# Input rows of an attention layer loaded in two-row parts, and the statistics rows asked for one unit earlier

## The chip, the cores and the metric

The kernel runs on one core of a Trainium2 chip. Its measure is the device time in microseconds (us) of one execution: 2961.36 us, the median of three runs (2960.82 to 2961.66). The engines of the core are named as the profile names them: PE is TensorE's matrix multiply and PEld its weight load, DVE is VectorE, ACT is ScalarE, POOL is GpSimd, SP is SyncE, which here only issues transfers. An engine followed by q (SPq) is its sequencer.

## The reference

The input x is 2 images of 128 channels by 256 x 256 pixels in float32 (a row of all channels is 128 KB). Two layers follow each other, each a normalisation over groups of four channels, a function, and the addition of the layer's input:

```python
x = x + attention(group_norm(x))   # layer 0: 8x8 windows, keys of a 12x12 halo, 4 heads, fixed mask
x = x + convolutions(group_norm(x))   # layer 1: 5x1, then 3x1 by channel, times a 3-tap product
```

In layer 0 the pixels are projected to queries, keys and values with a 384 x 128 matrix; a window of 8 x 8 queries attends to the 12 x 12 keys around it, with relative position terms, a mask that leaves only keys of the query's own row and column parity, and a softmax; the result is projected with a 128 x 128 matrix. A group's mean and variance go over 4 channels and all 65,536 pixels, so no pixel of an image can be normalised before all of it has been read once.

## The kernel before

Both layers go over an image in 32 strips of 8 rows, so there are 64 strips. In layer 0 a strip `k` has two units, `u = 2k + r`, one for even and one for odd rows (the mask keeps them apart); 128 units follow each other. One unit is a fixed sequence on PE: biases (L562), scores (L579), keys of a later unit (L382), coefficients (L473), weighted values (L605), then in an even unit (r = 0) the values of the next strip (L495), in an odd unit the queries of two units (L445, L447), and the output projection (L382). All engines run in the order in which the program was written: the loop stands in `manual_schedule(engines=ORDERED)`, so nothing is moved by a scheduler. A transfer that SP issues waits for all that SP has been told before it.

What SP is told in layer 0, in order:

- even unit: `load_rows(k + 2)`, the ten input rows of the strip after next (L316, 1280 KB, tile `f_raw`, three buffers); after `values` the transfers of `bring(0, ...)` (L525, L529, L532), which copy the values from one SBUF tile (`f_vn`) into the places from which L605 reads them (`f_vt`); then the store of this unit's result (L643, 512 KB).
- odd unit: `load_next()` (L305), then `bring(1, ...)` after `attend`, then the store.

`load_next` serves the statistics of the second image: while the first image is attended, its rows are read into a single buffer (`f_sx`) and VectorE takes their sums (`input_stats`, L128). This is done 29 times, ten rows each in the first 12 and eight rows each in the other 17, in the even units 2 to 58 (`stats_at`). The buffer is filled again from the odd unit after that. The rows of the first image are read for statistics before the loop (L266), at the start of the kernel.

A `bring` has six transfers, or twelve where the strip's four key rows are put in two pieces. With three strips to a turn, the twelve-transfer `bring(1, ...)` falls into units 3, 9, 15 and so on, just ahead of the even units 4, 10, 16. Each transfer of SP counts on one of eight semaphores in turn, and waits until the transfer before it on that semaphore has landed.

A unit's `normalise(k + 2)` (DVE, L356) in the odd unit reads the ten rows that were asked for in the even unit before it. Layer 1 has loads and stores of its own and isn't touched by the change.

Of the kernel before, what the change touches and what calls it, by code (L numbers as in the profile page):

```python
# [187 lines left out]
def attention_fast(tc, io, x1_d, norm, st_x, st_y, tags, ends, weights, both, layer1):  # L188

    nc = tc.nc  # L190
    x = io["x"]
# [3 lines left out]
    with ExitStack() as l0:  # L195
# [43 lines left out]
        with ExitStack() as setup:  # L239
# [24 lines left out]
            for s in range(NS):  # L264
                t = sp.tile([P, 8, W], F32, tag="sx", name=f"f_sx_0_{s}")
# [16 lines left out]
        stats_at, norm_at = {}, {}  # L282
        quarter_at = {}
        for b in range(NB - 1):
            row = 0
            for i in range(NS - 3):
                n = 10 if i < 12 else 8
# [9 lines left out]
        coming, sxs = sorted(stats_at), {}  # L297

        def load_next():
            if coming:  # L300
                u = coming.pop(0)
                b, row, n = stats_at[u]
                t = rawp.tile([P, 10, W], F32, tag="sx", name=f"f_sx_{b}_{row}", bufs=1)
                sxs[u] = t[:, 0:n]
                nc.sync.dma_start(sxs[u], x[b, :, row : row + n, :])  # L305

        def input_stats(u):
            b, row, n = stats_at[u]
# [2 lines left out]
        def load_rows(k):  # L311

            b, s = divmod(k, NS)
            t = rawp.tile([P, 10, W], F32, tag="raw", name=f"f_raw_{k}")
            n = min(10, H - 8 * s)
            nc.sync.dma_start(t[:, 0:n, :], x[b, :, 8 * s : 8 * s + n, :])  # L316
            raws[k] = t

        def slots_of(k):

            first = (4 * k + 2) % 6
            return [(0, 4, first)] if first < 4 else [(0, 2, 4), (2, 2, 0)]
# [78 lines left out]
        def keys(u, first=TWO, second=TWO):  # L401
            k, r = divmod(u, 2)
            s = k % NS
            keys_r = by_window(r)

            def part(c):
                pk = ps_pj.tile([P, 512], F32, tag="pj", name=f"f_pk_{u}_{c}")
                in_parts(second if c else first, pk, wkT, xn[k % 2][:, :, r, c].rearrange("p n i j -> p n (i j)"))
                for i, m, slot in slots_of(k):
                    nc.scalar.copy(  # L410
                        keys_r[:, c, :, 8 * slot : 8 * (slot + m)],
                        pk.rearrange("p (n x) -> p n x", n=NPAIR)[:, :, 8 * i : 8 * (i + m)],
                    )
                if c:
                    for i, m, slot in slots_of(k):
                        beside(r, slot, m)

            def top():

                pk = ps_pj.tile([P, 512], F32, tag="pj", name=f"f_pk_{u}_top")  # L420
                for c in range(2):
                    nc.tensor.matmul(
                        pk[:, W * c : W * c + W], wkT,
                        tops[k // NS][1][:, :, r, c].rearrange("p n i j -> p n (i j)"), start=True, stop=True,
                    )
                slot = (4 * k) % 6
                nc.scalar.copy(
                    keys_r[:, :, :, 8 * slot : 8 * slot + 16],
                    pk.rearrange("p (c n x) -> p c n x", c=2, n=NPAIR),
                )  # L430
                beside(r, slot, 2)

            return ([top] if s == 0 else []) + [lambda c=c: part(c) for c in range(2)]
# [70 lines left out]
        def top_values(b):  # L504

            flat, _, v = tops[b]
            for g in range(2):
                pv = ps_pj.tile([P, 512], F32, tag="pj", name=f"f_pv_top_{b}_{g}")
                for n in range(4):
                    nc.tensor.matmul(  # L510
                        pv[:, P * n : P * n + P], flat[:, P * (4 * g + n) : P * (4 * g + n) + P], wvT,
                        start=True, stop=True,
                    )
                (nc.vector.tensor_copy if g % 2 else nc.scalar.copy)(
                    v[:, 4 * g : 4 * g + 4, :, 0:32], pv.rearrange("p (n h d) -> p n h d", n=4, h=HEADS)
                )
# [19 lines left out]
        def bring_top(r, b):  # L536

            v, slot = tops[b][2], 4 * NS * b % 6
            for c in range(2):
                for odd in range(2):  # L540
                    lo, to = 64 * odd + 16 * (2 * r + c), 64 * c
                    nc.sync.dma_start(
                        vt[r][to + 8 * slot : to + 8 * slot + 16, c, odd:NPAIR:2], v[lo : lo + 16]
                    )
                    first = to + 48 + 2 * slot
                    nc.sync.dma_start(
                        vt[r][first : first + 3 : 2, c, odd + 1 : NPAIR : 2], v[lo + 7 : lo + 16 : 8, 0 : 8 - odd]
                    )
                    nc.sync.dma_start(
                        vt[r][first + 1 : first + 4 : 2, c, 1 - odd : NPAIR - 1 : 2],  # L550
                        v[lo : lo + 9 : 8, 1 - odd : 8],
                    )
# [98 lines left out]
        def emit(parts):  # L651
            for f in parts:
                f()

        load_rows(0)
        load_rows(1)
        weights.load()
        with tc.manual_schedule(engines=ORDERED):
            normalise(0)
            emit(keys(0, ONE, ONE))  # L660
            top_values(0)
            bring_top(0, 0)
            values(0, range(4))
            for r in range(2):
                bring(r, slots_of(0))
            bring_top(1, 0)
            by_place(0, (0, 4))
            coefficients(0, 0)
            coefficients(0, 1)
            normalise(1)  # L670
            by_place(1, (0, 2))
            for u in range(2):
                emit(queries(u, ONE, ONE))
            for u in range(NU):
                k, r = divmod(u, 2)
                b, s = divmod(k, NS)
                later, more = u + 1 < NU, k + 1 < NB * NS
                if r == 0:
                    if k + 2 < NB * NS:
                        load_rows(k + 2)  # L680
                elif k + 2 < NB * NS:
                    normalise(k + 2)
                if u in stats_at:
                    input_stats(u)
                if u == 0 or u - 1 in stats_at:
                    load_next()
                step = lambda: None
                if u in norm_at:
                    st, i, name = norm_at[u]
                    steps = norm.steps(st[i], ps_pj, name, last=False)  # L690
                    step = lambda: next(steps)
                if u == 8:
                    weights.sums()
                if u in (NU - 4, NU - 2, NU - 1):
                    next(layer1)
                biases(u)
                scores(u, pieces(u)[3])
                step()
                step()
                at_top = more and (k + 1) % NS == 0  # L700
                cuts = pieces(u)[0]
                if later:
                    emit(keys(u + 1, cuts, cuts))
                step()
                step()
                if more:
                    coefficients(k + 1, r)
                elif later:
                    next(layer1)
                step()  # L710
                attend(u)
                if more and r == 1:
                    bring(1, slots_of(k + 1))
                    if at_top:
                        bring_top(1, b + 1)
                if not later:
                    next(layer1)
                turn(u)
                step()
                if r == 0 and more:  # L720
                    if at_top:
                        top_values(b + 1)
                        bring_top(0, b + 1)
                    values(k + 1, range(4))
                    bring(0, slots_of(k + 1))
                elif later and more:
                    cuts = pieces(u)[1]
                    emit(queries(u + 1, cuts, cuts) + queries(u + 2, cuts, cuts))
                if more and r == 0:
                    by_place(k + 1, (2, 4))  # L730
                elif k + 2 < NB * NS:
                    by_place(k + 2, (0, 2))
                if u > 0:
                    result_stats(u - 1)
                project(u)
                if u in quarter_at:
                    st, i, name, part = quarter_at[u]
                    norm.quarter(st[i], name, part)
                del qs[u]
            result_stats(NU - 1)  # L740
# [966 lines left out]
```

## Time and profile before

| | |
|---|---|
| median of three runs | 2961.36 us |
| the profiled execution, its own time | 2962.31 us |
| its span, first to last instruction | 2960.0 us |
| granted PE clock, mean | 0.993 |
| layer 0, from unit 0 to the start of unit 127 | 113.27 to 1955.97 us |
| PE busy in that stretch | 1771.95 of 1842.70 us |
| DVE, ACT, POOL busy in that stretch | 1149.15, 894.61, 560.92 us |
| share of DMA time in that stretch, rate | 0.56, 150 GB/s |
| rest, layer 1: PE busy | 989.84 of 1004.03 us |

How to read it: the span is one execution as the hardware profiler saw it. Busy times of engines overlap. The instructions that PE and PEld execute are counted apart (51,762 each). A wait of an engine is put down to what ended it; "issue" means that nothing the profile shows ended it. In the list of DMA queues, q1 carries what SP issues, q0 what POOL issues, and q8 and q14 carry instructions to the engines. In answers on stretches of time, each number before a bracket is busy time of an engine in us.

### The profile page before, as it was taken

Reading aid. Unit: us, or ns where it says so; the run is one execution under the profiler, and the core shown is the slowest. Engines: PE = TensorE matmul, PEld = TensorE weight load, DVE = VectorE, ACT = ScalarE, POOL = GpSimd, SP = SyncE. Lnnn points to the kernel's source line nnn. Section 1 sums busy time; section 2 is a strip of 40 time slices with the busy share of each in tenths; the row PEclk is TensorE's granted clock in tenths of the full one; section 3 lists DMA queues with packets and bytes.
Section 4 is the critical chain, followed back from the end, with each engine's and each line's share of the span. In section 5 each row is a group of like instructions: output and inputs, shape, how many; then the busy total and the mean of one; then the engine's idle time right before and its main releaser. Section 6 shows DMA issues by size and latency. Waiting matters only on the chain.

```text
span 2960.0 us, 117321 instructions
## 1 busy us (share of the span) xinstructions
PE 2780.9 (94%) x51762; PEld 2106.9 (71%) x51762; DVE 2136.9 (72%) x3601; ACT 1511.8 (51%) x2379; POOL 641.1 (22%) x2049
## 2 busy tenths in 40 slices
PE   0698999999999999999999999999999999999998
PEld 0488888888888888999999999964444444444443
DVE  8556666666666656565565566579999999999997
ACT  0343444444545444544554554546666655666654
POOL 1223222323223323323323333300000000000000
PEclk9999999999999999999999999999999999999999
DMA  9655656565656555554555555548788877888885
GB/s 394 199 163 139 175 172 172 162 168 160 168 166 187 133 128 136 139 128 137 145 129 140 142 129 138 133 122 219 215 219 218 219 209 209 221 218 217 218 217 148
DMA packets 157844, 521.83 MB, mean 176 GB/s; under 512 B 20784, under 2 KB 98064, under 8 KB 117008
## 3 DMA queue, kind: packets, MB, share of 16 engines
q1 hardware_dynamic: 148256, 448.17, 51.3%
q0 software_dynamic: 9072, 66.06, 11.9%
q8 instruction: 412, 6.75, 0.9%
q14 instruction: 104, 0.85, 0.1%
HBM read 284.78 MB, written 134.22 MB: 142 GB/s over the span
## 4 chain that ended last, share of the span: by engine, by line
PE 92%; issue 5%; DVE 1%; ACT 1%; POOL 1%; DMA 1%; SPq 0%; DVEq 0%; ACTq 0%; POOLq 0%
PE a_o L887 11%; PE a_e L887 11%; PE f_s L579 9%; PE f_o L605 8%; PE f_pk L382 8%; PE f_pv L495 8%; PE f_py L382 8%; PE f_pq L447 6%; PE f_pa L473 5%; PE f_s L562 5%; PE a_d L938 4%; PE f_pq L445 2%; PE b L980 2%; PE a_c L887 2%; PE g L867 2%
## 5 line engine op out<-in xcount | busy, mean ns | idle before, releaser
L589 ACT ACTIVATE f_p<-f_s 128x512 f32<-128x512 f32 x512 | 265.9, 604 | 444.6 <-PE f_s L579 444.6
L486 DVE TENSOR_SCALAR f_cf<-f_pa,f_keep 128x512 f32<-128x512 f32 x128 | 103.7, 810 | 537.0 <-ACT f_cf L482 536.9
L453 ACT ACTIVATE f_q<-f_pq,f_head 128x512 f32<-128x512 f32 x512 | 304.9, 704 | 158.2 <-PE f_pq L447 158.1
L396 POOL COPY f_kt<-f_kt 128x60 f32<-128x60 f32 (+1 forms) x348 | 106.0, 340 | 1257.3 <-ACT f_kt L410 1233.5
L373 POOL COPY f_xq<-f_xn 128x96 f32<-128x96 f32 x1024 | 333.4, 356 | 8.5 <-DVE f_xn L356 8.5
L962 ACT ACTIVATE t<-t,w 128x1024 f32<-128x1024 f32 x127 | 146.1, 1151 | 367.2 <-DVE t L955 362.7
L969 DVE SCALAR_TENSOR_TENSOR t<-t,w,t 128x1024 f32<-128x1024 f32 x254 | 325.9, 1283 | 7.5 <-ACT t L962 1.3
L579 PEld LDWEIGHTS f_s<-f_q,f_kt 64*64 64x64 f32 x17176 | 274.7, 133 | 69.9 <-issue 69.9
L579 PE MATMUL f_s<-f_q,f_kt 64*64 64x64 f32 (+1 forms) x17176 | 293.8, 222 | 19.3 <-issue 19.3
L605 PE MATMUL f_o<-f_vt,f_p 128*32 128x66 f32 x16384 | 273.0, 220 | 25.7 <-issue 25.6
L605 PEld LDWEIGHTS f_o<-f_vt,f_p 128*32 128x32 f32 x16384 | 245.9, 108 | 40.4 <-issue 31.4
L382 PE MATMUL f_pk<-f_xn,f_wqkvT 128*128 128x192 f32 (+3 forms) x1496 | 261.4, 325 | 0.7 <-ACT f_kt L410 0.7
L998 POOL DMA_DIRECT2D y<-f_x x63 | 54.6, 866 | 918.7 <-DVE y L990 871.2
L495 PE MATMUL f_pv<-f_wqkvT,f_xn 128*128 128x128 f32 x2048 | 246.9, 278 | 4.9 <-issue 4.9
L382 PE MATMUL f_py<-f_ot,f_woT 128*128 128x160 f32 (+1 forms) x1520 | 248.6, 314 | 2.2 <-DVE f_ot L623 1.8
L887 PE MATMUL a_o<-xm,w1s 128*128 128x512 f32 x512 | 242.2, 594 | 4.7 <-ACT t L878 4.7
L495 PEld LDWEIGHTS f_pv<-f_wqkvT,f_xn 128*128 128x128 f32 x2048 | 234.0, 192 | 11.6 <-issue 5.7
L887 PE MATMUL a_e<-xm,w1s 128*128 128x512 f32 x512 | 240.7, 591 | 0.0
L382 PEld LDWEIGHTS f_py<-f_ot,f_woT 128*128 128x128 f32 x1520 | 232.3, 193 | 4.3 <-ACT xm L808 1.9
L382 PEld LDWEIGHTS f_pk<-f_xn,f_wqkvT 128*128 128x128 f32 x1496 | 224.7, 192 | 12.9 <-issue 1.7
L447 PE MATMUL f_pq<-f_xn,f_wq_s 128*128 128x192 f32 (+1 forms) x1008 | 211.3, 331 | 3.2 <-issue 3.0
L612 DVE TENSOR_TENSOR f_on<-f_o,f_rc 128x320 f32<-128x320 f32 (+1 forms) x384 | 197.1, 513 | 13.3
(149 smaller groups left out, 4662.9 us busy)
## 6 DMA issues: line engine op xcount, KB each, us to landing
f_raw<-in_x SPq DMA_DIRECT2D x62, 1280.0 KB
f_x<-f_x SPq DMA_DIRECT2D x128, 512.0 KB
y<-f_x POOLq DMA_DIRECT2D x63, 1024.0 KB, 7.8
out<-y SPq DMA_DIRECT2D x63, 1024.0 KB
f_sx<-in_x SPq DMA_DIRECT2D x49, 1024.0 KB
f_vt<-f_vn SPq DMA_DIRECT2D x172, 264.0 KB
raw<-f_x SPq DMA_DIRECT2D x64, 640.0 KB
raw<-f_x SPq DMA_DIRECT2D x62, 384.0 KB
```

The costliest lines, as they stand in the source:

```text
L373: nc.gpsimd.tensor_copy(xq[:, half, t2, 1:4, :, c].rearrange("p t r n e -> p r t n e"), xn[k % 2][:, windows, :, c, 0:3, t2:8:4].rearrange ...
L382: nc.tensor.matmul(dst[:, 512 * lo // last : 512 * hi // last], w, moving[:, n * lo // last : n * hi // last], start=True, stop=True,)
L447: nc.tensor.matmul(by_pair[:, lo:hi, 8:32], wq_s, xn[k % 2][:, lo:hi, r, c, 0:3].rearrange("p n i j -> p n (i j)"), start=True, stop=True,)
L453: nc.scalar.activation(q[:, c, :, i].rearrange("p n (j t) -> p n j t", t=4), pq.rearrange("p (n t j) -> p n j t", n=NPAIR, t=4), AF.Copy, ...
L473: nc.tensor.matmul(pa[64 * half : 64 * half + 64, 64 * t : 64 * t + 64], wb[:, t2, t1].rearrange("p h x -> p (h x)"), xq[:, half, t2, t1]. ...
L495: nc.tensor.matmul(pv[:, P * n : P * n + P], xn[k % 2][:, 4 * g + n].rearrange("p r c i j -> p (r c i j)"), wvT, start=True, stop=True,)
L579: nc.tensor.matmul(sc[g][n // 8][64 * c : 64 * c + 64, n % 8, lo:hi].rearrange("p i x -> p (i x)"), kt[r][rows, c, NKEY * n : NKEY * n + 6 ...
L589: nc.scalar.activation(pts[u][:, g, 8 * half : 8 * half + 8].rearrange("p n i x -> p (n i x)"), sc[g][half].rearrange("p n i x -> p (n i x ...
L605: nc.tensor.matmul(po[32 * h : 32 * h + 32, n - lo], p[:, h // 2, n, h % 2], vt[r][:, :, n, h], start=True, stop=True,)
L612: nc.vector.tensor_tensor(on[:, :, lo:hi].rearrange("p c n d -> p n c d"), po[:, :, :, 0:32], rc.to_broadcast([P, hi - lo, 2, 32]), ALU.mult,)
L887: nc.tensor.matmul(pa[:, : n * W], w, rows, start=i == 0, stop=i == len(terms) - 1)
L969: nc.vector.scalar_tensor_tensor(t3[:, j : j + 4], t1[:, j + tap : j + tap + 4, :], w3[:, tap : tap + 1], t3[:, j : j + 4], ALU.mult, ALU.add,
```

## The change

Three things change, all in layer 0. A load of a strip's rows (from strip 2 on) becomes five transfers of two rows, 256 KB each, in place of one of 1280 KB; where a strip has eight rows, four. A load of statistics rows becomes five or four such transfers too. And `load_next` is called in the even unit itself, straight after that unit's `input_stats`, and so behind the strip's rows in SP's order, no longer in the odd unit that follows. The reading instructions, their number and their order on PE, DVE, ACT and POOL stay as they are.

```diff
@@ load_next
                 sxs[u] = t[:, 0:n]
-                nc.sync.dma_start(sxs[u], x[b, :, row : row + n, :])
+                for lo in range(0, n, 2):
+                    nc.sync.dma_start(t[:, lo : lo + 2], x[b, :, row + lo : row + lo + 2, :])
@@ load_rows
             n = min(10, H - 8 * s)
-            nc.sync.dma_start(t[:, 0:n, :], x[b, :, 8 * s : 8 * s + n, :])
+            m = n if k < 2 else 2
+            for lo in range(0, n, m):
+                nc.sync.dma_start(t[:, lo : lo + m], x[b, :, 8 * s + lo : 8 * s + lo + m, :])
@@ the loop over units
                 if u in stats_at:
                     input_stats(u)
-                if u == 0 or u - 1 in stats_at:
+                if u == 0 or u in stats_at:
                     load_next()
```

## The prediction

> **What bounds the kernel now.** I read the page's busy times and DMA queues first. PE is busy 94% of the span, so only its idle time and its throttled time can be won.
>
> ```profile
> PE 2780.9 (94%) x51762; PEld 2106.9 (71%) x51762; DVE 2136.9 (72%) x3601; ACT 1511.8 (51%) x2379; POOL 641.1 (22%) x2049
> ...
> q1 hardware_dynamic: 148256, 448.17, 51.3%
> ...
> q8 instruction: 412, 6.75, 0.9%
> ```
>
> The last row matters: 412 packets of 16 KB. PE and PEld execute 103,524 instructions, 251 for each packet: q8 brings TensorE its program, on the same DMA engines as the data. Next, the waits, of the engines and then of SP's queue:
>
> ```profile
> PEld f_s L579 <- issue: 69.9, 138, 4.1
> ...
> DVE st_x L128 <- DMA f_sx<-in_x: 28.8, 10, 5.2
> ```
>
> ```profile
> SPq L529 <- DMA f_sx<-in_x: 44.9, 10, 7.2
> ```
>
> PE's stalls in layer 0 are nearly all "issue": no engine released them. One of them, unit 10, in the timeline, with the DMA queues of two stretches around its end (276.8 to 279.9, then 279.9 to 281.6):
>
> ```profile
> 270.21 0.62 SPq L305 DMA_DIRECT2D f_sx<-in_x  x1
> ...
> 277.85 1.49 PE L579 MATMUL f_s<-f_q,f_kt 64*64 64x32 f32 x77
> ...
> 281.68 0.58 SPq L529 DMA_DIRECT2D f_vt<-f_vn  x1
> ...
> 282.75 1.76 PE L579 MATMUL f_s<-f_q,f_kt 64*64 64x64 f32 x53 [3.40 <-issue]
> ```
>
> ```profile
> q1 hardware_dynamic: 72, 0.30, 78.5%
> ...
> q1 hardware_dynamic: 34, 0.12, 33.6%
> q8 instruction: 1, 0.02, 5.8%
> ```
>
> PE stops in the middle of the scores at 279.3. No instruction packet starts until the statistics load of 270.2 and the bring behind it have nearly drained; one then does, and PE goes on at 282.75. So I read the stalls as late instruction fetches behind bulk data. To price this I cut layer 0 at the first L562 of each unit and asked for sums over six sets of units: A, even units behind a twelve-transfer bring, with statistics (10); B, other even units with statistics (20); C, odd units 3 to 59 (29); then the same three kinds from unit 72 on, where no statistics are loaded, D (9), E (18), F (26). Columns: total time, then busy times.
>
> ```profile
> sum 173.27, PE 149.03 PEld 136.26 DVE 99.57 ACT 59.32 POOL 48.90; mean PE 14.90 PEld 13.63 DVE 9.96 ACT 5.93 POOL 4.89
> ...
> sum 286.77, PE 278.29 PEld 255.11 DVE 191.96 ACT 106.25 POOL 91.75; mean PE 13.91 PEld 12.76 DVE 9.60 ACT 5.31 POOL 4.59
> ...
> sum 418.12, PE 403.37 PEld 370.71 DVE 285.84 ACT 246.22 POOL 122.08; mean PE 13.91 PEld 12.78 DVE 9.86 ACT 8.49 POOL 4.21
> ...
> sum 123.30, PE 123.30 PEld 114.00 DVE 64.35 ACT 51.47 POOL 42.98; mean PE 13.70 PEld 12.67 DVE 7.15 ACT 5.72 POOL 4.78
> ...
> sum 258.34, PE 250.45 PEld 229.42 DVE 129.44 ACT 100.97 POOL 83.07; mean PE 13.91 PEld 12.75 DVE 7.19 ACT 5.61 POOL 4.61
> ...
> sum 356.43, PE 356.43 PEld 329.56 DVE 249.73 ACT 213.75 POOL 107.16; mean PE 13.71 PEld 12.68 DVE 9.61 ACT 8.22 POOL 4.12
> ```
>
> Per unit: A 17.33, B 14.34, C 14.42; D 13.70, E 14.35, F 13.71. Three readings. The floor of a unit is 13.70, PE never idle. B equals E, although B does 2.5 us more on DVE: the statistics arithmetic costs nothing, and what B and E lose (0.65) they lose beside the strip's own rows. The statistics loads cost in C (0.71 each) and most in A (3.63 each), the units after an odd one in which a bring queues behind the load.
>
> **What the Trainium skill says.** "Runtime: NRT & Kernel Launch", Instruction fetch mechanics: instructions come in 16 KiB blocks of 256 on a DMA queue of their own; "mostly hidden", it says. The packet count agrees, the 3.40 us does not. "DMA: Bandwidth & Descriptors", Queues, rings and completion order: a DMA engine takes turns between queues only at packet borders, so a fetch can sit behind a whole packet of a load; unit 10 fits, but the trace doesn't show what a packet border of a load is. "TensorE: Matmul & The Clock Gate", Part 1: the clock halves after an idle window of about 3.4 us; unit 10 has 19.37 us against 13.70 plus 3.69 idle, so some 2 us went to a lower clock. The DMA page's Rules for kernel authors ask for 1 MiB or more per transfer, which speaks against the change; no run here shows 256 KB loads from x.
>
> **The change part by part.**
>
> 1. Odd units lose the statistics load. C should become F: 418.12 - 29 x 13.71 = 20.5 us won. DVE's 28.8 us of waiting for these rows goes too, but B = E says it wasn't on the path; I count nothing.
> 2. Nothing then stands before the twelve-transfer bring, and the strip's rows behind it start earlier (SP's 44.9 us of waits go). A should become D: 173.27 - 10 x 13.70 = 36.3 us.
> 3. Even units now carry up to 2560 KB. At the 350 GB/s that q1 held over 302.3 to 306.4, a part of 262 KB takes 0.75 us, ten parts 7.5. The ten rows in one load took 3.7. What a fetch waits for a part isn't in the trace: at least nothing, at most one part (0.75) if turns are taken between transfers, and the whole 7.5 if they are not. I take turns between transfers. A fetch then loses at most 0.75 in place of 3.7, and B's 0.65 should shrink; with a fetch due every 4.9 us (95,893 PE and PEld instructions in layer 0's 1842.7 us, 256 each), so two in the loaded stretch, I leave 0.4 per even unit, 30 x 0.4 = 12.0. A and B together: 36.3 + (286.77 - 20 x 13.70 = 12.8) - 12.0 = 37.1 us.
> 4. Rows in parts where no statistics are loaded: about 21 units of kind E from 62 on, 0.65 each, of which I take half: 7 us.
> 5. Units 0 and 1 take 36.69 us, 9.3 above two floors, and unit 65 takes 19.72, 6.0 above, with a row load in flight in each: 3 us for each of the two, by the same halving or less.
>
> Costs. SP issues 345 more transfers (246 for strips, 99 for statistics) at 0.62 us, the length of L305 and L316 issues: 214 us, over 64 pairs of units of 27.4 us in which SP issued about 22 transfers (13.6 us) and now issues 30 (18.6). In an even unit the parts are issued from 1.5 us in (2.7 in A) to 7.7 (8.9); the values' bring is issued at 12.8 to 14.6 and waits for VectorE's copies anyway. That cover lasts even if SP is held to the drain: 1.5 + 1.5 for the store ahead (512 KB at 350 GB/s) + 7.5 = 10.5, in A 11.7. The statistics parts wait for VectorE's L128 reads of the same unit, which run until 3.8 us in; SP arrives there at 4.6, so nothing is queued behind a new wait. If it came late, the bring and then the store would follow late, with a unit to spare. With the eight semaphores, a bring's first transfer waits for the part eight before it: landed by then. Readers wait on four more semaphores a strip, at 28 ns each (the semaphore instructions at L305), 7 us of DVE time in all, hidden under DVE's idle 28%. I price all of these at nothing; if SP's cover were gone, each late bring would cost as in A, which is rival two.
>
> Sum: 20.5 + 37.1 + 7 + 6 = 70.6. From the profiled execution's 2962.31 (span 2960.0 and 2.3 around it) that leaves 2891.7; the median stands 0.95 lower, so 2890.8, rounded to 2891.
>
> **Rivals.**
>
> One, half the gain: parts don't let a fetch in, because SP has up to eight of them queued, as much as one load before. Then the even units lose B's 0.65 twice, 15.0 each: 30 x 15.0 = 450 against 460.0, 10 won, and with step 1's 20.5 the time is 2961.4 - 30.5 = 2931. For it: store and loads already hold the engines full for 5 us in even units (1792 KB at 350 GB/s). Against: B's loss is small though a whole load stands there.
>
> Two, slower: the double load keeps every fetch of the even unit waiting. If each of 30 even units then costs what A costs now, 17.33, they take 519.9, 59.9 more, less 20.5 from the odd ones: 3001. It decides from a mean of 460.0 + 20.5 = 480.5 / 30 = 16.0 us per even unit. For it: unit 10's fetch waited for an almost complete drain. Against: the drain there was of a load and a bring mixed, and these are now apart by some 2 us.
>
> Three, no change: the stage is slow from VectorE's extra work or the transfers are hidden, so moving them does nothing, 2961. B = E speaks against it. That the parts are not issued is excluded: SP's instruction order shows them.
>
> **How the numbers follow.** Forecast 0.72 (2871 to 2912), rival one 0.19 (2912 to 2945), two 0.05, three 0.04. The bottom is every term at its full size: 20.5 + 49.1 + 14 + 6 = 90 won, 2871. The top takes in rival one, 2932. A measurement of this kernel tells 0.2%, about 6 us, from no change. Faster 0.92, same 0.03, slower 0.05.
>
> **What would show it.** Right: odd units of 13.7, PE never idle; the L579 stalls by "issue" gone from units 4, 10, 16; no SP wait at L529 for f_sx and no DVE wait for it at L128; even units with statistics near 14.1. Rival one: even units near 15, stalls by "issue" at L605 and L495. Rival two: 16 or more. Wrong altogether: stalls that stay where they are although no load is in flight; or a bring that comes late, seen as PE waiting at L605 for f_vt.

## The result, and the profile after

The changed kernel takes 2913.64 us, the median of four runs (2907.39 to 2921.27); the kernel before, beside it, 2961.09 (2957.96 to 2961.66). The ratio is 0.984, with a 95% interval of 0.982 to 0.987. The forecast was 2891 with a range of 2871 to 2932: the sign and the range hold, but 47 us were won where 70 were forecast. (The prediction gave 2871 to 2912 to its forecast and 2912 to 2945 to rival one; the time lies 1.6 us inside rival one's part.) The profiled execution took 2912.66 us, with a span of 2910.7 against 2960.0.

First the busy times and the DMA queues of the page of the kernel after (queues: packets, MB, share of 16 engines' span):

```profile
PE 2766.5 (95%) x51762; PEld 2095.5 (72%) x51762; DVE 2134.0 (73%) x3601; ACT 1506.9 (52%) x2379; POOL 643.1 (22%) x2049
...
q1 hardware_dynamic: 197936, 448.19, 53.1%
...
q8 instruction: 412, 6.75, 1.0%
```

TensorE executes as many instructions as before, with the same 412 instruction packets; the data are the same, in more packets. PE is busy 14.4 us less although it does the same work: part of what was lost had been counted as busy. Next, the waits of PE in layer 0 that no engine ended, first in the kernel before (total us, times, longest us), then, with one of PEld, in the kernel after:

```profile
PE f_o L605 <- issue: 25.6, 34, 4.1
PE f_s L579 <- issue: 19.3, 10, 4.0
PE f_pq L445 <- issue: 14.6, 8, 3.2
...
PE f_pv L495 <- issue: 4.9, 4, 2.2
```

```profile
PE f_o L608 <- issue: 14.1, 23, 1.5
PE f_pv L498 <- issue: 9.4, 17, 1.4
...
PEld f_s L582 <- issue: 49.2, 128, 0.4
```

Before, PE stood still in the scores ten times, for up to 4.0 us; now it doesn't, and PEld's longest wait there is 0.4. What is left is short stalls at the weighted values (L608) and the values (L498), nearly all in even units. SP's wait of 44.9 us for `f_sx` at L529 and VectorE's of 28.8 us for the second image's rows at L128 are gone. Unit 10, which had the 3.40 us stall in its scores, now begins at 259.73. In its timeline (start, length, engine, line, operation, tiles, count):

```profile
260.77 2.19 PE L582 MATMUL f_s<-f_q,f_kt 64*64 64x32 f32 x130
...
262.40 3.92 SPq L319 DMA_DIRECT2D f_raw<-in_x  x5
...
265.93 2.05 PE L608 MATMUL f_o<-f_vt,f_p 128*32 128x66 f32 x128
...
266.43 2.28 SPq L306 DMA_DIRECT2D f_sx<-in_x  x5
```

The scores run through; SP asks for the five row parts and then for the five statistics parts while PE works. An even unit that still stalls is unit 14 (315.37 to 330.76). PE stands still before 323.23 for 1.03 us:

```profile
323.23 1.69 PE L608 MATMUL f_o<-f_vt,f_p 128*32 128x66 f32 x101 [1.03 <-issue]
```

The DMA queues from 316.9 to 320.9, and then from 320.9 to 321.9:

```profile
q1 hardware_dynamic: 789, 1.01, 82.7%
...
q1 hardware_dynamic: 161, 0.29, 87.3%
q8 instruction: 1, 0.02, 5.9%
```

No instruction packet starts in the first stretch; one starts 5.6 us into the unit, and PE goes on 2.3 us after its start. It is the picture of before with a shorter delay. The six sums over units, taken and named as in the prediction (A, B, C with statistics in the kernel before; D, E, F without; the same order):

```profile
sum 143.38, PE 138.89 PEld 127.26 DVE 97.70 ACT 56.99 POOL 49.14; mean PE 13.89 PEld 12.73 DVE 9.77 ACT 5.70 POOL 4.91
...
sum 287.47, PE 278.72 PEld 255.23 DVE 195.64 ACT 113.05 POOL 92.36; mean PE 13.94 PEld 12.76 DVE 9.78 ACT 5.65 POOL 4.62
...
sum 397.73, PE 397.73 PEld 367.71 DVE 281.25 ACT 238.22 POOL 122.45; mean PE 13.71 PEld 12.68 DVE 9.70 ACT 8.21 POOL 4.22
...
sum 124.55, PE 123.75 PEld 114.03 DVE 65.43 ACT 51.24 POOL 43.16; mean PE 13.75 PEld 12.67 DVE 7.27 ACT 5.69 POOL 4.80
...
sum 257.80, PE 250.37 PEld 229.40 DVE 129.22 ACT 100.78 POOL 83.40; mean PE 13.91 PEld 12.74 DVE 7.18 ACT 5.60 POOL 4.63
...
sum 356.87, PE 356.74 PEld 329.70 DVE 249.20 ACT 213.56 POOL 107.41; mean PE 13.72 PEld 12.68 DVE 9.58 ACT 8.21 POOL 4.13
```

| stretch | before, us | after, us | won | forecast |
|---|---|---|---|---|
| C, 29 odd units | 418.12 | 397.73 | 20.4 | 20.5 |
| A, 10 even units behind a long bring | 173.27 | 143.38 | 29.9 | 32.3 |
| B, 20 other even units | 286.77 | 287.47 | -0.7 | 4.8 |
| E, 18 even units from 72 on (forecast: 21 from 62 on) | 258.34 | 257.80 | 0.5 | 7 |
| units 0 and 1 | 36.69 | 32.82 | 3.9 | 3 |
| unit 65 | 19.72 | 20.18 | -0.5 | 3 |
| all else (span) | | | -4.2 | 0 |
| sum | | | 49.3 | 70.6 |

Odd units run at the floor. A fell from 17.33 to 14.34 a unit, and not by idle time alone: 19.8 us are PE's idle time (24.2 to 4.5), 10.1 its busy time, for the same work. In units 4, 10, 22 and 34 the granted clock of PE was 0.85, 0.91, 0.91 and 0.90 before; after, it is 1.00 in all ten. Unit 10 before and after (window; busy us of PE, PEld, DVE, ACT, POOL with counts; granted clock, DMA share, GB/s):

```profile
276.81:296.18 19.37, 15.68 (x380) 14.38 (x379) 10.21 (x20) 5.93 (x12) 4.84 (x17) 0.91 0.52 130
```

```profile
259.73:273.71 13.98, 13.85 (x379) 12.73 (x378) 10.12 (x20) 5.70 (x12) 4.87 (x17) 1.00 0.80 243
```

B did not move, but it now carries the statistics loads as well. E, where nothing changed but the split of the rows, stands at 14.32 against 14.35.

### The profile page after: what moved, and what is told of

The parts are those of the page before. It is cut to its first block, busy times and chain, and to the rows that moved or that the text cites. A ratio compares the mean times of both kernels' runs of the same rounds, so it can differ in the third digit from the quotient of the medians.

```text
span 2910.7 us, 117791 instructions
## 1 busy us (share of the span) xinstructions
PE 2766.5 (95%) x51762; PEld 2095.5 (72%) x51762; DVE 2134.0 (73%) x3601; ACT 1506.9 (52%) x2379; POOL 643.1 (22%) x2049
## 4 chain that ended last, share of the span: by engine, by line
PE 77%; issue 18%; POOL 1%; DVE 1%; SPq 1%; DMA 1%; ACT 1%; POOLq 0%; DVEq 0%; ACTq 0%
PE f_s L582 9%; PE f_o L608 8%; PE f_pk L385 8%; PE f_pv L498 8%; PE f_py L385 8%; PE a_o L890 6%; PE a_e L890 6%; PE f_pq L450 6%; PE f_pa L476 5%; PE f_s L565 5%; PE f_pq L448 2%; PE a_d L941 2%; PE a_c L890 1%; PE b L983 1%; PE g L870 1%
## 5 line engine op out<-in xcount | busy, mean ns | idle before, releaser
L582 PE MATMUL f_s<-f_q,f_kt 64*64 64x64 f32 (+1 forms) x17176 | 287.8, 220 | 0.0
L608 PE MATMUL f_o<-f_vt,f_p 128*32 128x66 f32 x16384 | 269.6, 220 | 14.2 <-issue 14.1
L608 PEld LDWEIGHTS f_o<-f_vt,f_p 128*32 128x32 f32 x16384 | 244.3, 108 | 27.2 <-issue 18.0
L498 PE MATMUL f_pv<-f_wqkvT,f_xn 128*128 128x128 f32 x2048 | 251.0, 279 | 10.9 <-issue 9.4
L498 PEld LDWEIGHTS f_pv<-f_wqkvT,f_xn 128*128 128x128 f32 x2048 | 235.4, 192 | 20.2 <-issue 13.4
```

The source lines that it names most:

```text
L498: nc.tensor.matmul(pv[:, P * n : P * n + P], xn[k % 2][:, 4 * g + n].rearrange("p r c i j -> p (r c i j)"), wvT, start=True, stop=True,)
L582: nc.tensor.matmul(sc[g][n // 8][64 * c : 64 * c + 64, n % 8, lo:hi].rearrange("p i x -> p (i x)"), kt[r][rows, c, NKEY * n : NKEY * n + 6 ...
L608: nc.tensor.matmul(po[32 * h : 32 * h + 32, n - lo], p[:, h // 2, n, h % 2], vt[r][:, :, n, h], start=True, stop=True,)
```

## The experiments

The kernels ran in three groups, each on one chip beside the kernel before. That took 2967.14 us (median) beside the move alone, the parts alone, and the two kernels without late rows and without the store; 2973.1 beside the whole rows, the store behind the rows, the one-row parts, and the kernel before without the store; and 2957.83 beside the last three. Ratios are therefore compared across these groups, and times within one. The sums over units come from one profiled execution each. Where kernels share the program of the units, they show the scatter: A and B together took 430.9 us in the changed kernel, 432.7 and 433.6 in two that differ from it only from strip 36 on; E took 14.35, 14.49 and 14.52 a unit in three kernels with whole rows. The diffs are against the changed kernel, with lines between left out ("...").

### One part of the change alone

The move alone, with whole loads:

```diff
-                for lo in range(0, n, 2):
-                    nc.sync.dma_start(t[:, lo : lo + 2], x[b, :, row + lo : row + lo + 2, :])
+                nc.sync.dma_start(sxs[u], x[b, :, row : row + n, :])
...
-            m = n if k < 2 else 2
-            for lo in range(0, n, m):
-                nc.sync.dma_start(t[:, lo : lo + m], x[b, :, 8 * s + lo : 8 * s + lo + m, :])
+            nc.sync.dma_start(t[:, 0:n, :], x[b, :, 8 * s : 8 * s + n, :])
```

> Statistics rows asked for in even units behind the strip's rows, but both loads whole, as before. Theory P (parts let an instruction fetch in, whole loads keep it out): odd units with statistics fall to 13.7 us, but the even ones now hold a fetch behind up to 2560 KB in two loads, 15.5 us or more each against 14.36 in the changed kernel, so 2945 us or more. Theory M (taking the load from in front of the brings is the whole gain, parts do nothing): even units as in the changed kernel, 14.3 to 14.4, and a time within 6 us of its 2914.

Measured: 2934.53 us (2933.43 to 2937.14), ratio 0.989 (0.987 to 0.991). PE's waits in this kernel, and its sums over A, B and C:

```profile
PE f_pv L495 <- issue: 28.5, 28, 1.7
PE f_o L605 <- issue: 20.2, 26, 4.4
```

```profile
sum 148.30, PE 138.87 PEld 127.26 DVE 97.73 ACT 56.96 POOL 49.11; mean PE 13.89 PEld 12.73 DVE 9.77 ACT 5.70 POOL 4.91
...
sum 300.01, PE 279.28 PEld 255.28 DVE 195.80 ACT 113.05 POOL 92.43; mean PE 13.96 PEld 12.76 DVE 9.79 ACT 5.65 POOL 4.62
...
sum 397.54, PE 397.54 PEld 367.59 DVE 281.09 ACT 238.23 POOL 122.48; mean PE 13.71 PEld 12.68 DVE 9.69 ACT 8.21 POOL 4.22
```

The move alone gives all of C and 25.0 of A's 29.9, and costs 13.2 in B (14.34 to 15.00 a unit): each of the 28 even units in which statistics rows are asked for (2 to 56) now stalls at the values. Even units of 14.9 on average lie between the two expectations, 15.5 and 14.3 to 14.4. The parts alone, with `load_next` left in the odd unit:

```diff
-                if u == 0 or u in stats_at:
+                if u == 0 or u - 1 in stats_at:
```

> Both loads in two-row parts, but the statistics rows asked for in odd units, as before. Theory P: a fetch waits for a part at most, so the odd units fall from 14.42 to about 13.9 and the A units from 17.33 to 15 or less: 2925 us or less. Theory M: the brings still queue behind the load, C stays near 14.4 and A near 17, 2955 to 2965 us.

Measured: 2934.28 us (2926.50 to 2940.61), ratio 0.989 (0.987 to 0.992). The sums over A and C:

```profile
sum 150.02, PE 142.09 PEld 129.82 DVE 97.84 ACT 58.47 POOL 49.11; mean PE 14.21 PEld 12.98 DVE 9.78 ACT 5.85 POOL 4.91
...
sum 404.75, PE 399.90 PEld 367.83 DVE 283.74 ACT 242.34 POOL 122.54; mean PE 13.79 PEld 12.68 DVE 9.78 ACT 8.36 POOL 4.23
```

A is 15.00 a unit, C 13.96, B 14.38. Parts alone take out most of A's loss and over half of C's without any move, as the first expectation had it, though its time of 2925 or less was not reached. Each half of the change is worth 1.1%, both together 1.6%. They overlap in A, where each alone wins 23 to 25 us of the 29.9, and in C, where the move has all and the parts alone 13.4; in B the parts undo what the move costs. With the rows whole again, and the move and the statistics in parts kept:

```diff
-            m = n if k < 2 else 2
+            m = n
```

> The changed kernel with whole loads for the strip's rows; the statistics rows are in parts and in even units. If the rows' cut does nothing: E 14.3 to 14.4, A and B as in the changed kernel (14.35), a time within 6 us of 2914. If it does part of the work: A and B between 14.4 and the 14.9 to 15.0 of the run with both loads whole, 2920 to 2930.

Measured: 2931.32 us (2929.06 to 2935.53), ratio 0.987 (0.984 to 0.990). The sums over A and B:

```profile
sum 147.78, PE 138.88 PEld 127.26 DVE 97.75 ACT 56.98 POOL 49.09; mean PE 13.89 PEld 12.73 DVE 9.77 ACT 5.70 POOL 4.91
...
sum 300.96, PE 279.12 PEld 255.33 DVE 195.91 ACT 113.05 POOL 92.38; mean PE 13.96 PEld 12.77 DVE 9.80 ACT 5.65 POOL 4.62
```

A is 14.78, B 15.05: the same as with everything whole. The split of the statistics rows does nothing if the rows ahead of them are whole. The split of the rows is worth 0.44 in A (14.78 to 14.34) and 0.68 in B (15.05 to 14.37), 18 us over these 30 units. In E it is worth 0.2 at most (14.52 here, 14.49 with the move alone and 14.35 before, against 14.32), which is about the scatter.

### What holds the fetch where there are no statistics

E shows what is left with the least beside it: a store of 512 KB, and behind it the rows. Two kernels take one of the two away, from strip 36 on. First no row loads:

```diff
-        coming, sxs = sorted(stats_at), {}
+        coming, sxs, kept = sorted(stats_at), {}, {}
...
+            if k >= 36:
+                raws[k] = kept[k % 3]
+                return
             t = rawp.tile([P, 10, W], F32, tag="raw", name=f"f_raw_{k}")
+            kept[k % 3] = t
```

> The changed kernel without the loads of strip rows from strip 36 on: the rows of strips 33 to 35 are used again, so part of the input is left out. It asks what the E units (even, no statistics, 14.32 us, a stall at the weighted values) wait behind. If it is the strip's rows, E falls to 13.7 and 21 units win 13 us. If it is the store that the unit before left at the start of the even unit, or nothing in flight at all, E stays at 14.3 and its stalls of 0.4 to 0.9 us stay where they are.

Then the rows stay and no store stands ahead of them; an even unit's end issues two:

```diff
-            nc.sync.dma_start(x1_d[b][s][:, r:8:2, :], x1)
+            if k < 36 or k == 63:
+                nc.sync.dma_start(x1_d[b][s][:, r:8:2, :], x1)
+            elif r == 0:
+                for rr in range(2):
+                    nc.sync.dma_start(x1_d[b][s][:, rr:8:2, :], x1)
```

> The changed kernel with the stores of both units of a strip issued at the end of the even unit, from strip 36 on (the rows of the odd unit get the even unit's values, so half of the result rows are not the right ones). No store then runs at the start of an even unit, and two run at the start of an odd one. If E's stalls come from the store ahead of the fetch, E falls from 14.32 to 13.7 and the odd units rise above 13.71. If they come from the strip's rows or from nothing in flight, E stays at 14.3.

Measured, one run each: 2902.05 and 2902.03 us. The sum over E, without the rows and then without the store:

```profile
sum 246.25, PE 246.25 PEld 227.65 DVE 128.86 ACT 100.58 POOL 83.35; mean PE 13.68 PEld 12.65 DVE 7.16 ACT 5.59 POOL 4.63
```

```profile
sum 248.47, PE 247.74 PEld 228.30 DVE 128.93 ACT 100.83 POOL 83.60; mean PE 13.76 PEld 12.68 DVE 7.16 ACT 5.60 POOL 4.64
```

13.68 and 13.80 a unit against 14.32. Either transfer alone costs 0.1 or less; the store with the rows straight behind it costs 0.6. Without rows the first fetch of a unit of E starts 4.05 us into it on average, after the store; without the store at 4.09, while the row parts move. So parts do let a fetch in when nothing stands ahead of them. The same edit was made to the kernel before, with its whole rows (the diff is the same, against that kernel):

> The kernel before with the same move of stores as in the run without a store at the start of even units, from strip 36 on (half of the result rows are again not the right ones): whole loads of rows with no store ahead. If parts let a fetch in among the rows, E stays near 14.3 here, against 13.80 with parts. If the cut of the rows does not matter and only the store ahead does, E falls to 13.7 to 13.8 here too.

Measured, one run: 2979.72 us. PE's waits in it, and the sum over E:

```profile
PE f_o L605 <- issue: 44.0, 36, 4.6
```

```profile
sum 273.08, PE 250.87 PEld 229.60 DVE 132.00 ACT 100.71 POOL 82.96; mean PE 13.94 PEld 12.76 DVE 7.33 ACT 5.60 POOL 4.61
```

E rises to 15.17, which neither expectation had: with whole rows and no store the first fetch waits longer, until 5.84 us into the unit on average, when the load has nearly drained. The split is worth 1.37 a unit when the store isn't there and 0.2 at most when it is. In the kernel before, with the store ahead, the fetch starts at 4.93, while the whole rows still move; why it gets in there was not shown.

If the store is the trouble, an odd unit's store can go behind the rows of the next even unit:

```diff
-            nc.sync.dma_start(x1_d[b][s][:, r:8:2, :], x1)
+            held.append((x1_d[b][s][:, r:8:2, :], x1))
...
+        def store_held():
+            while held:
+                nc.sync.dma_start(*held.pop())
...
-                elif k + 2 < NB * NS:
-                    normalise(k + 2)
+                    store_held()
+                else:
+                    store_held()
+                    if k + 2 < NB * NS:
+                        normalise(k + 2)
...
+            store_held()
```

> The changed kernel with the store of the odd unit issued behind the strip's rows of the next even unit, ahead of the statistics rows; all work is done. If a fetch is held by a store and rows right behind it (the two looks before this one: E falls to 13.68 without rows, to 13.80 without the store), turning them round lets the fetch at 3.9 us into the unit through: E from 14.32 to about 13.8, 21 units at 0.5, some 10 us, and the stalls at the weighted values gone from B as well. Span about 2898, a ratio to the kernel before of about 0.980. If the order is indifferent, 2911 and 0.984.

Measured: 2909.75 us (2906.60 to 2923.63), ratio 0.980 (0.978 to 0.983). E falls to 13.88 and A to 13.94, but B rises to 14.66. PE's waits in it:

```profile
PE f_pv L499 <- issue: 13.1, 18, 1.4
PE f_o L609 <- issue: 8.6, 14, 1.4
```

Most of the stalls go from the weighted values to the values: the store now stands between the rows and the statistics rows, and it is the next fetch that is late (9.66 us into the units of B, 9.29 in the changed kernel).

### How large a part, and how fast SP asks

The rows and the statistics in parts of one row, 128 KB:

```diff
-                for lo in range(0, n, 2):
-                    nc.sync.dma_start(t[:, lo : lo + 2], x[b, :, row + lo : row + lo + 2, :])
+                for lo in range(n):
+                    nc.sync.dma_start(t[:, lo : lo + 1], x[b, :, row + lo : row + lo + 1, :])
...
-            m = n if k < 2 else 2
+            m = n if k < 2 else 1
```

> The changed kernel with parts of one row, 128 KB. If what a fetch waits for is the transfer under way, halving it shortens the wait: A and B from 14.35 to about 14.0, 10 us less in all, 2903. If it waits for what is queued on its engine, whatever its cut, A and B stay at 14.3 to 14.4; twice the transfers (20 in an even unit at 0.43 to 0.6 us each) then at best cost nothing, 2912 to 2925.

Measured: 2890.61 us (2888.32 to 2892.09), ratio 0.973 (0.971 to 0.976). A is 13.80, B 13.95, E 14.12. The middle of unit 14, from 4.5 to 9.5 us after its start, in the changed kernel and with one-row parts (columns as above):

```profile
319.87:324.87 5.00, 3.97 (x166) 3.48 (x164) 1.79 (x5) 1.85 (x3) 3.64 (x13) 1.00 0.98 347
```

```profile
315.74:320.74 5.00, 5.00 (x175) 4.67 (x174) 2.25 (x6) 1.87 (x4) 3.64 (x13) 1.00 0.80 229
```

With two-row parts the DMA engines are full, at 347 GB/s; with one-row parts they are at 0.80 and 229 GB/s. (In units 8, 12 and 18 the shares are 0.95 to 1.00 and 0.76 to 0.78.) Asking for a strip's rows takes SP 3.2 us in the E units of the changed kernel (1280 KB at 410 GB/s, more than the engines moved), and 6.2 with one-row parts (210 GB/s): some 0.6 us a part in both. So two things differ: the size of a transfer, and the pace at which SP asks for bytes. To part them, two-row parts were each followed by a transfer of 512 bytes:

```diff
+        pace, paced = rawp.tile([P, 96], F32, tag="pace", name="f_pace", bufs=1), []
+
+        def tiny():
+            i = len(paced) % 96
+            paced.append(i)
+            nc.sync.dma_start(pace[:, i : i + 1], x[0, :, 0, i : i + 1])
...
                     nc.sync.dma_start(t[:, lo : lo + 2], x[b, :, row + lo : row + lo + 2, :])
+                    tiny()
...
                 nc.sync.dma_start(t[:, lo : lo + m], x[b, :, 8 * s + lo : 8 * s + lo + m, :])
+                if k > 1:
+                    tiny()
```

> The changed kernel's parts of two rows, each followed by a transfer of 512 bytes (one column of x into a scratch tile), so that SP issues as many transfers as with one-row parts and has at most four parts under way, as many bytes as with eight one-row parts. If one-row parts gain because fewer bytes are queued and SP asks for them more slowly, this gains the same: A 13.8 and B 14.0 a unit, about 2891 us, ratio 0.973 or a little more. If they gain because each transfer is smaller, this stays at the two-row parts' A 14.34, B 14.37 and 2912 us, ratio 0.984. In between if both count.

Measured: 2895.14 us (2893.79 to 2900.04), ratio 0.978 (0.976 to 0.981). SP takes 5.8 us for a strip's rows. The same stretch of unit 14, and the sums over A and B:

```profile
316.49:321.49 5.00, 5.00 (x176) 4.67 (x175) 2.25 (x6) 1.97 (x4) 3.64 (x13) 1.00 0.76 217
```

```profile
sum 138.12, PE 137.56 PEld 126.91 DVE 98.14 ACT 57.18 POOL 49.12; mean PE 13.76 PEld 12.69 DVE 9.81 ACT 5.72 POOL 4.91
...
sum 283.72, PE 278.32 PEld 255.54 DVE 196.29 ACT 113.73 POOL 92.34; mean PE 13.92 PEld 12.78 DVE 9.81 ACT 5.69 POOL 4.62
```

A is 13.81, B 14.19, E 14.22. The expectation's third case came: both count. A and B together are 9.0 us shorter than in the changed kernel (430.9 to 421.8), where the next kernel, on the same chip with one-row rows, is 16.1 shorter. Slower asking, with transfers as large as before and tiny ones besides, gives about half, with a scatter of some 3 us in these sums. (The time comes closer; layer 1 took 3.7 us less than elsewhere in this profiled run, which nothing in the edit explains.) Whether it is the pace or the four parts under way that does it was not parted. Nor was, in the other half, the size of a transfer from that of its packets (2,048 bytes with two rows, 1,024 with one).

Only the rows in parts of one row, the statistics in two:

```diff
-            m = n if k < 2 else 2
+            m = n if k < 2 else 1
```

> The strip's rows in parts of one row, the statistics' rows in parts of two as in the changed kernel. If only what stands in the first five us of the unit counts, this has all of the one-row parts' gain: A 13.8, B 14.0, E 14.1, about 2891 us, ratio 0.973. If the statistics' parts count as well, the stalls at the values (12 us over A and B in the changed kernel, 0.6 with one-row parts) stay, and it gives about 2900 us, ratio 0.979.

Measured: 2889.82 us (2887.29 to 2893.04), ratio 0.976 (0.974 to 0.978). The sums over A and B:

```profile
sum 137.12, PE 137.12 PEld 126.78 DVE 97.61 ACT 56.81 POOL 48.88; mean PE 13.71 PEld 12.68 DVE 9.76 ACT 5.68 POOL 4.89
...
sum 277.64, PE 276.28 PEld 254.42 DVE 195.64 ACT 112.68 POOL 92.00; mean PE 13.81 PEld 12.72 DVE 9.78 ACT 5.63 POOL 4.60
```

A is 13.71, B 13.88, E 14.09, C 13.89 with three short stalls at the scores. In even units it has all of the gain of one-row parts: there only the rows' parts, in the first half of the unit, count. C is 5.0 us longer than with one-row parts throughout; by the intervals of the ratios the two kernels can't be told apart.

Last, one-row parts with the odd unit's store behind the rows: the two diffs of above together.

> Parts of one row, and the store of an odd unit issued behind the rows of the next even unit. If the two gains come from different places, they add where they were seen: E units go from 14.12 (one-row parts alone) to about 13.8 as they did with two-row parts (14.32 to 13.88), 20 to 30 even units gain 0.2 to 0.3 each, 5 us in all: 2885 us, ratio 0.971. If the one-row parts have taken what the later store took, the time is that of the one-row parts alone, 2890 us, ratio 0.973. If the later store pushes the values' fetch behind a longer unbroken stream, as with two-row parts (B rose to 14.66, stalls of 11.7 us at the values), B rises above 14.0 and the time is 2892 or more.

Measured: 2880.12 us (2878.01 to 2882.24), ratio 0.973 (0.970 to 0.975), 9.7 us under the kernel with one-row rows on the same chip, and no run of the one reaches a run of the other. It is faster than both kernels of this case. Its sums over B and E:

```profile
sum 274.93, PE 274.44 PEld 253.56 DVE 196.12 ACT 113.10 POOL 91.92; mean PE 13.72 PEld 12.68 DVE 9.81 ACT 5.66 POOL 4.60
...
sum 246.20, PE 246.20 PEld 227.61 DVE 128.98 ACT 100.61 POOL 83.33; mean PE 13.68 PEld 12.64 DVE 7.17 ACT 5.59 POOL 4.63
```

Every one of the six sets of units is at the floor or within 0.05 of it. With two-row parts the later store had moved the stall on; with one-row parts the second fetch comes in time too. What is still lost lies outside the sets: unit 65 takes 21.56 us, more than before (19.72), and unit 126 15.24 (12.29). In unit 65 PE waits 2.92 us for VectorE's `f_x`.

The next table puts the kernels side by side. The middle columns are means of my own over the trace's packet records, us into the unit: the start of the second instruction packet in B and of the first in E, not counting those of the first 2 us. The others are us a unit. Left out are the kernels altered only from strip 36 on, the parts alone, and the kernel with whole rows and the statistics rows in parts.

| kernel | second fetch in B | first fetch in E | A | B | E |
|---|---|---|---|---|---|
| before | 8.39 | 4.93 | 17.33 | 14.34 | 14.35 |
| move alone | 10.04 | 5.05 | 14.83 | 15.00 | 14.49 |
| the change | 9.29 | 4.94 | 14.34 | 14.37 | 14.32 |
| store behind the rows | 9.66 | 4.18 | 13.94 | 14.66 | 13.88 |
| paced two-row parts | 9.16 | 4.99 | 13.81 | 14.19 | 14.22 |
| one-row parts | 8.42 | 4.78 | 13.80 | 13.95 | 14.12 |
| one-row rows | 8.25 | 4.69 | 13.71 | 13.88 | 14.09 |
| one-row parts, store behind | 7.72 | 3.61 | 13.71 | 13.75 | 13.68 |

In the E units the first fetch starts at 4.9 to 5.1 with rows whole, in two-row parts, or paced, and at 4.7 to 4.8 with one-row parts. It moves by more when the store moves. In B a later second fetch goes with a longer unit in all the kernels of the table that have the statistics in even units.

## Why the prediction was right or wrong

**The bound.** Right. The stalls by "issue" are late instruction fetches. The place of the stalls shows it: counting the records of PE, PEld and PE's sequencer up to a stall, all 413 such stalls of PE over 0.3 us in layer 0, in the thirteen kernels profiled, stand 192 or 193 past a multiple of 256, and there is one fetch packet for 255 of these records (105,101 and 412). In all 413, PE went on 2.2 to 4.1 us after the start of the last packet (median 2.4). And the stalls shrank where the data stream was broken up, moved where it was reordered, and all but three vanished in the last kernel, while the instructions of PE stayed the same:

```profile
PE f_o L609 <- issue: 5.6, 3, 2.8
```

**Step 1, C to F.** Right: 20.4 us against 20.5; the move alone shows all of it, 13.71 a unit.

**Step 2, A to D.** Right in kind: no scores stall is left in A, and A won 29.9 where 36.3 less the residual of step 3 was forecast (32.3). The prediction's reading of unit 10, some 2 us lost to a lower clock, fits its granted clock of 0.91 before and 1.00 after.

**Step 3, the residual in even units.** Its size was wrong. It said that a fetch loses at most one part, 0.75 us, and left 0.4 a unit, 12.0 in 30 units. Measured against the same floor, A and B keep 143.38 + 287.47 - 411.0 = 19.9, 0.66 a unit, so 7.9 us of the miss lie here. The term that was mis-sized is the wait for a part: the second fetch starts at 9.29 in B, and at 7.72 in the last kernel; if nothing delays it there, it loses 1.6 us on average, two parts. The step took turns between transfers as the rule; in these runs a turn came later than after one part. That SP asks faster than the engines move, or has too many parts under way, is part of the cause, for slower asking, which changes both, gave about half of what one-row parts gave; how the turns are taken was not shown. Its mechanism, that splitting the rows helps the even units, holds: 0.44 to 0.68 a unit against whole rows. (Of B's twenty units one, unit 60, has no statistics, and B's VectorE does 2.4 us more than E's, not 2.5; neither moves the argument.)

**Step 4, 7 us where no statistics are loaded.** Wrong: E won 0.5. The step took the row load as the cause of E's 0.65. The runs show two causes that, with rows in parts, need each other: without the rows E is at the floor, without the store nearly so. With the store ahead, splitting the rows changes the fetch's start from 4.93 to 4.94. Why a store followed by row parts delays the fetch, when either alone doesn't, was not settled.

**Step 5.** Units 0 and 1 won 3.9 for 3. Unit 65 won nothing for 3: its stall of 4.1 us at the weighted values fell to 0.5, as the step said, but then PE waited 4.0 us at L448 for coefficients from VectorE (`f_cf`), which had been hidden behind the stall:

```profile
PE f_pq L448 <- DVE f_cf L489: 5.4, 2, 4.0
```

A floor taken from other units didn't hold for a unit that does more.

**Costs.** Pricing them at nothing was right. SP's issue of a part took mostly 0.43 to 0.63 us, with some of 0.9 to 1.9; no PE wait for `f_vt` appeared. VectorE's wait for `f_raw`, two waits in both kernels, went from 10.0 to 11.5 us. Left unpriced were small losses: D 1.3, unit 126 1.9 (its granted clock was 0.88, against 1.00 before), the rest 1.0, 4.2 in all beside unit 65. What in them is the change and what scatter was not tried.

**The sum.** The gap of 21.3 us: steps 2 and 3 together 7.9 (2.4 in A, 5.5 in B), step 4 6.5, unit 65 3.5, all else 4.2, less 0.9 won more at the start.

**The rivals.** Rival one gave 15.0 for an even unit, 2931 us; measured was 14.36 for A and B. Its size was wrong, but its sign came, stalls at the weighted values and the values, and its mechanism, that SP has too much queued, fits what was left: halving the parts, and with them the bytes of eight, brought the ratio from 0.984 to 0.973, and slower asking with parts of two rows gave about half of that in the even units. That the range held is owed to its top, which had been set to take in this rival. Rival two needed 16.0; even with both loads whole it was 14.9, so it is excluded. Rival three is excluded by C alone.

The Trainium skill ("DMA: Bandwidth & Descriptors", Rules for kernel authors) was named as speaking against the change, since it asks for 1 MiB or more per transfer where maximum bandwidth is the goal. Here smaller transfers were better: 1280 KB, then 256 KB, then 128 KB parts, all with the move, gave ratios of 0.989, 0.984 and 0.973. Bandwidth isn't the goal in this layer: its DMA share was 0.56 before, and the kernel whose DMA engines moved 229 GB/s in the stretch above is faster than the one with 347.

## What to carry to other kernels

Where PE stalls by "issue" in the middle of a long unrolled sequence, compare the instruction queue's packets with the bulk transfers: a load that nobody waits for can stop PE by holding back its program. What helped here was to split such loads until SP asked for them more slowly than the engines can move, and then to put a store behind them and not ahead. Read the stage again after each step, for the stall can move to the next fetch, as it did when the store was moved with two-row parts. And when a step's gain is taken from "the stall goes", ask in each unit what would end the wait then; in unit 65 VectorE was 4.0 us late behind it.

## What the runs showed of the hardware

- Late instruction fetches of TensorE cost here tens of us: 2960.0 us of span before against 2880.3 in the last kernel, with the same PE instructions, the same data and the same 412 packets. A fetch packet itself takes 0.9 to 1.8 us in most cases, and where PE stood still for one, it went on 2.2 us or more after the packet's start, 2.4 in the median.
- A unit loses more than the idle time shows: in E after the change PE is idle 7.4 us of 257.8, but the units are 11.6 longer than in the last kernel; the other 4.2 us are longer busy time of PE for the same work, at a granted clock of 1.00. In A before, a granted clock of 0.85 to 0.91 came on top in four of ten units.
- Moving a transfer out of the way made a stage slower: with no store ahead, whole row loads delayed the fetch by more (5.84 against 4.93 us, 14.35 to 15.17 a unit).
- A two-row part of 256 KB is issued by SP in 0.43 us when nothing holds it back, less than the 0.62 of the whole load before; one after the other, parts of 256 and of 128 KB both came out every 0.6 us or so.
